# Values and output projection of two token tiles at once, by seven part products from blocks kept in DRAM

## The chip, the cores and the metric

The kernel runs on one core of a Trainium2 chip. The metric is the device time of one execution in microseconds (us): 2246.51 us before the change, the median of three runs (2245.76 to 2247.95).

## What is computed

Eight batches of 1024 tokens with 512 features go through a layer norm, then through attention with 16 heads of 32 features and through a gate with weights of plus and minus one. All of it is float32.

```python
xn = layernorm(x)                                   # x: (8, 1024, 512)
q, k, v = (heads(xn @ W.T + b) for W, b in ...)     # 16 heads of 32
scores = q @ k.T / sqrt(32)                         # masked where i % 256 < j % 256
attn = softmax(scores) @ v
s = attn @ Wo.T + bo
g = silu(clip((xn @ sign(fw).T) * scale + bias, -100, 100))
out = x + s * g
```

## The kernel before

**Tiles.** Tokens are taken in tiles of 128 (`it` = 0 to 7 of a batch `b`), heads in groups of four (`g` = 0 to 3). Every float32 product is issued as four matmuls of 32 output rows each, which lie side by side in TensorE's columns (`product`, L339); 512 columns wide, such a set of four is one of four chunks of a product, and the planner books it at 0.86 us (L382, L405). `values_work` (L373) makes the values of one token tile: four chunks into one PSUM bank, then one copy by ScalarE (L377). `output_work` (L711) makes the output of one token tile: four chunks, then on VectorE the bias (L722) and the gate (L723), on GpSimd the residual (L724), and a DMA out (L725).

**Steps.** The attention runs in 288 steps, nine for each batch and head group (L1053). In a step, `probs_quad` (L571) computes scores into a PSUM tile of four banks, called `t`, and ScalarE takes the exponential of it (L612); `attend_quad` (L618) multiplies the probabilities of the step before with the values; `maxima_quad` (L494) computes the scores `s` of the next head group into a PSUM tile of the same pool, and VectorE reduces them to maxima (L528). That pool, `ps_q`, has one buffer (L111): `t` cannot be started before the reduction of the previous `s` has ended, nor `s` before the exponential of `t`.

**What fills the gaps.** Between `t` and `s`, and between `s` and the next `t`, TensorE gets other work: the products for q, k, the values V, the output O, the gate G, and transposes. The strings STEADY, OPENING and CLOSING (L787 to L804) give the order of this filler work for each batch and head group; `V4` is the values of token tile 4, a stroke marks the batch after. `Beside.fill` (L919) deals it out: 1.2 us of booked cost between `t` and `s` (L1094), and at least 2.35 or 2.45 us between `s` and the next `t` (L1126). Works that cost no TensorE time are put off (`kept`, L1095) until after the reduction has been issued (L1122).

**Buffers and queues.** All filler products share two PSUM banks (`ps_t`, L113). GpSimd adds the probabilities of the steps up (L643); a probability tile, of which there are two (L104), comes free when that add has read it. The head groups' results `aT` are divided by VectorE (L700, four reciprocals of 128 columns) and multiplied (L704). All loads and stores of the loop are issued on SP's queue. Each engine runs its instructions in the order in which the code emits them.

Of the kernel before, what the change touches and what calls it, by code (L numbers as in the profile page):

```python
# [9 lines left out]
F32 = mybir.dt.float32  # L10
# [63 lines left out]
def tile_gated_window_attention(  # L74
# [27 lines left out]
    qk = pool("qk", 3)  # L102
    heads = pool("heads", 6)
    probs = pool("probs", 2)  # L104
    total = pool("total", 1)
    tmp = pool("tmp", 5)
    parts = pool("parts", 1)
    rows_p = pool("rows", 1)
    small = pool("small", 4)
    spill = pool("spill", 2, space=bass.MemoryType.DRAM)  # L110
    ps_q = pool("ps_q", 1, space=PSUM)  # L111
    ps_a = pool("ps_a", 2, space=PSUM)
# [128 lines left out]
    def turn_weight(name):  # L241


        def turn(c):
            if c == 0:
                wT[name] = const.tile(
                    [P, NC, D], F32R if name == "fw" else F32, name=f"{name}T"
                )
            dst = wT[name]
            if name == "wk" and c % 2:  # L250

                ps = ps_a.tile([P, 512], F32, tag="av", name=f"wkT_{c}")
            else:
                ps = bank(f"{name}T_{c}")
            for o in range(NC):
                nc.tensor.transpose(
                    ps[:, o * P : (o + 1) * P], staged[name][o][:, c * P : (c + 1) * P], ident
                )
            if name == "fw":

                sg = temp(f"sign_{c}")
                nc.vector.tensor_scalar(sg, ps, 0.0, 2.0, ALU.is_ge, ALU.mult)
                nc.vector.tensor_scalar(dst[:, c, :], sg, -1.0, None, ALU.add)
            elif name == "wo":

                nc.scalar.mul(dst[:, c, :], ps, 0.5)
            elif name == "wk":
                nc.scalar.copy(dst[:, c, :], ps)
            else:
                evacuate(dst[:, c, :], ps)  # L270

        return [lambda c=c: turn(c) for c in range(NC)]


# [97 lines left out]

    def values_work(b, it):  # L373
        def after(ps):

            vt[b, it] = vpool.tile([P, D], F32, tag="v", name=f"v_{b}_{it}")
            nc.scalar.copy(vt[b, it], ps)  # L377

        return product(
            f"v_ps_{b}_{it}",  # L380
            [(lambda c=c: (xn_cols(b, it)[:, c, :], wT["wv"][:, c, :])) for c in range(NC)],
            0.86,  # L382
            after,
            lambda: (b, it) in turned,
        )

    def heads_work(b, g, half, which):
# [20 lines left out]
        )  # L408

    def gate_work(b, it, plain=False):  # L410

# [4 lines left out]

        def split():
            src = xn_cols(b, it)
            for i in range(2):
                part[i] = parts.tile([P, NC, P], F32R, tag=f"x{i}", name=f"x{i}_{b}_{it}", bufs=2)  # L420
            nc.scalar.copy(part[0], src)  # L421
            nc.gpsimd.tensor_tensor(part[1], src, part[0].bitcast(F32), ALU.subtract)  # L422
# [21 lines left out]
        def passes(i):  # L444
# [3 lines left out]
            for c in range(NC):  # L448
# [3 lines left out]
                )  # L452
            if i:
                after(hold[0])

# [22 lines left out]
        )  # L478
        split = Work(0, split, ready=lambda: (b, it) in turned)
        return split, [main], squash, finish  # L480


# [215 lines left out]
    def invert(b, g, f, part):  # L698
        r = aT[b, g, f][:, part * P : (part + 1) * P]
        nc.vector.reciprocal(r, r)  # L700

    def normalise_heads(b, g, f, part=None):
        cols = slice(0, HALF) if part is None else slice(part * P, (part + 1) * P)
        nc.vector.tensor_tensor(  # L704
# [3 lines left out]

    back = {}

    def output_work(b, it):  # L711
# [7 lines left out]
        def after(ps):  # L719
# [6 lines left out]

        pairs = [
            (lambda g=g: (aT[b, g, it // 4][:, (it % 4) * P : (it % 4 + 1) * P], wT["wo"][:, g, :]))
            for g in range(NC)
        ]  # L730
        return fetch, product(f"o_ps_{b}_{it}", pairs, 0.86, after, lambda: it in back, True)

    def last_output(b, it):
# [8 lines left out]
        def rest():  # L742
            for part, queue in enumerate((nc.sync, nc.scalar)):
                at = slice(part * 256, part * 256 + 256)
                ps = bank(f"o_ps_{b}_{it}_{part}")
                for g in range(NC):
                    for h in range(NH):
# [3 lines left out]
                            lhsT=aT[b, g, it // 4][:, cols],  # L751
                            rhs=wT["wo"][:, g, at],
                            start=(g == 0),
# [9 lines left out]
    def row_work():  # L763
# [7 lines left out]
        def after(ps):  # L771
            nc.vector.scalar_tensor_tensor(rows["bo"], rows["bo"], 0.5, ps, ALU.mult, ALU.add)

        return spread, product(
            "bo_ps", [(lambda c=c: (wide[0][:, c, :], wT["wo"][:, c, :])) for c in range(NC)], 0.86, after,
            lambda: bool(wide), True,
        )
# [7 lines left out]


    STEADY = (  # L787
        "V4 G2 V5 q20 | V7 G3 V6 k20 q21 G4 k21",
        "O4 G5 O5 | q30 N0 k30 O6 q31 G6 k31 G7",
        "N1 O7 O0 | O1 k00' V0' q00' O2 O3 q01'",  # L790
        "k01' V1' | q11' G0' V2' k10' G1' V3' k11' q10'",
    )
    OPENING = (
        "V2 G0 V3 V4 G1 V5 V7 V6 G2 k20 q21 k21",
        "G3 q20 q30 N0 k30 | G4 q31 G5 k31 G6 V0'",
        "G7 N1 V1' | k00' q00' W0 V2' W1 V3' W2 q01' W3",
        "k01' G0' R | q11' k10' G1' k11' q10'",
    )
    CLOSING = (
        "V4 V5 | q20 V7 V6 k20 q21 k21",  # L800
        "O4 O5 | q30 k30 O6 q31 O7 k31",
        "H2 O0 H3 O1 H4 O2 H5 O3 H6 H7 |",
        "-",
# [15 lines left out]

    blocks, links = [], []  # L820

    def link(i, fn, tail=False):
        links.append((i, fn, tail))

    def plan(b, g, text):
        for word in text.split():
# [24 lines left out]
            elif kind in "qk":  # L851
                main = heads_work(bb, int(number[0]), int(number[1]), kind)
            elif kind == "V":
                main = values_work(bb, int(number))
            elif kind == "W":
                main = [Work(0.5, turn_weight("wo")[int(number)], edge=True)]
            elif kind == "R":
                spread, main = row_work()
                link(i - 3, spread)
            elif kind == "O":  # L860
                fetch, main = output_work(b - 1, int(number))
                link(i - 1, fetch)
            else:
                split, main, squash, finish = gate_work(bb, int(number), kind == "H")
                if split is not None:
                    link(i - 3, split)
                later = 1 if b in (0, B - 1) else 0
                link(i + 2 + later, squash)
# [163 lines left out]

    wv_turns, fw_turns = turn_weight("wv"), turn_weight("fw")
    start = heads_work(0, 0, 1, "k")
    start += woven(heads_work(0, 1, 1, "q"), wv_turns[:2])
    start += woven(heads_work(0, 1, 0, "k"), wv_turns[2:])
    start += values_work(0, 0)
    start += woven(heads_work(0, 1, 1, "k"), fw_turns[:2])
    start += woven(heads_work(0, 1, 0, "q"), fw_turns[2:])
    start += values_work(0, 1)  # L1040
    start = Beside(start, [0] * NQ)
# [12 lines left out]
    for s, (b, g, n) in enumerate(steps):  # L1054
# [12 lines left out]
        def fill(want, kept=None, turns=1):  # L1067

            spent = 0.0
            for one in line:  # L1070
                if spent < want - 0.1:
                    spent += one.fill(want - spent, kept, one is not now, turns)
                if one.work:
                    break
# [17 lines left out]
        if first:  # L1092
            shift_rows(*turn)
        want = max(1.2 - mine, 0.0) if nxt else share  # L1094
        spent = fill(want, kept, 0)  # L1095
        if nxt and spent < want - 0.5:
            spent += fill(want - spent, kept)
        share -= spent
        if turn and not first:
# [49 lines left out]
    for i, it in enumerate(order):  # L1149
# [8 lines left out]
        if it == order[-2]:  # L1158
            ahead, rest = last_output(b, order[-1])
            ahead()  # L1160
        for w in units[it][1]:
            w.run()

# [44 lines left out]
```

## Time and profile before

| What | us |
|---|---|
| median of three runs | 2246.51 |
| the profiled execution itself | 2248.59 |
| its span, first to last instruction | 2246.7 |
| steps begin at | 80.1 |
| a batch in the steady state (from the first `t` of one to that of the next) | 271.3 to 271.8 |
| one step of these, mean | 7.5 |
| exponential of a full `t` (L612) | 1.88 |
| reduction of a full `s` (L528, 128x2048) | 2.29 |

The span divides into 80 us of preparation, 288 steps, and some 35 us of output for the last batch. An engine's busy time is the union of its instructions; TensorE's matmuls overlap, so the mean duration of one matmul in a row is more than what it adds to the time. How far apart sets of four start is the better measure, and it is read from the timeline.

### The profile page before, as it was taken

The numbers are of one execution on the slowest core, as the hardware profiler recorded it, in microseconds if no ns is written. First come the engines' busy times: TensorE is split into PE (matmuls) and PEld (weight loads), VectorE is DVE, ScalarE is ACT, GpSimd is POOL, SyncE is SP. The second block draws the span as 40 slices with busy tenths as digits, with TensorE's granted clock in tenths as the row PEclk, the third lists the DMA queues.
The fourth block names the chain that finished last, engine by engine and source line by source line (L and its number), as shares of the span: only waits on it lengthen the run. The fifth ranks groups of instructions, "written<-read, shape, count | busy, mean of one in ns | idle before, by whom it ended". The sixth has DMA issues, their size and how long they took to land. (4 is left out here: it accounts for less than half of the span.)

```text
span 2246.7 us, 56396 instructions
## 1 busy us (share of the span) xinstructions
PE 2196.6 (98%) x25553; PEld 851.8 (38%) x25553; DVE 1276.6 (57%) x1633; ACT 876.5 (39%) x864; POOL 1323.7 (59%) x1198
## 2 busy tenths in 40 slices
PE   8999999999999999999999999999999999999998
PEld 3334333343333433333333333334333343333333
DVE  4556556665556655566555665565655665555664
ACT  2235433434334434344333443334334344333331
POOL 1256566666566666576556665557666566655562
PEclk9999999999999999999999999999999999999999
DMA  4001000120001210012000120002100111000113
GB/s 164 1 16 34 11 6 29 53 76 30 25 25 39 72 33 25 25 62 68 16 25 25 62 67 16 25 26 66 62 16 27 41 62 62 7 20 25 44 53 123
DMA packets 49672, 93.55 MB, mean 42 GB/s; under 512 B 5388, under 2 KB 5656, under 8 KB 49432
## 3 DMA queue, kind: packets, MB, share of 16 engines
q1 hardware_dynamic: 48720, 88.76, 12.0%
q8 instruction: 200, 3.28, 0.6%
q10 hardware_dynamic: 712, 1.19, 0.2%
q14 instruction: 40, 0.33, 0.0%
HBM read 56.37 MB, written 33.55 MB: 40 GB/s over the span
## 5 line engine op out<-in xcount | busy, mean ns | idle before, releaser
L643 POOL TENSOR_TENSOR p<-p,p 128x512 f32<-128x512 f32 x930 | 1096.4, 1212 | 202.7 <-PE av L625 111.2
L528 DVE TENSOR_REDUCE pm<-s 128x4 f32<-128x2048 f32 (+3 forms) x384 | 664.9, 1752 | 608.8 <-PE s L515 605.9
L612 ACT ACTIVATE p<-t 128x2048 f32<-128x2048 f32 x288 | 540.9, 1878 | 856.4 <-PE t L599 797.8
L700 DVE RECIPROCAL aT<-aT 128x128 f32<-128x128 f32 x256 | 230.2, 928 | 222.4 <-ACT aT L661 222.4
L515 PE MATMUL s<-k,q 32*128 32x512 f32 (+3 forms) x3072 | 320.2, 510 | 7.8 <-ACT p L612 6.9
L625 PE MATMUL av<-p,v 128*32 128x512 f32 (+3 forms) x3072 | 308.2, 496 | 1.6 <-DVE aT L704 1.4
L599 PE MATMUL t<-q,k 32*128 32x512 f32 (+3 forms) x3072 | 306.1, 492 | 0.0
L351 PE MATMUL q_ps<-xnT,wqT 128*32 128x512 f32 (+2 forms) x2656 | 254.2, 497 | 5.5 <-ACT xnT L322 4.7
L351 PE MATMUL k_ps<-xnT,wkT 128*32 128x512 f32 (+2 forms) x2784 | 257.2, 487 | 1.1 <-ACT xnT L322 0.7
L351 PE MATMUL v_ps<-wvT,xnT 128*32 128x512 f32 (+3 forms) x2712 | 254.9, 491 | 0.0
L351 PE MATMUL o_ps<-woT,aT 128*32 128x512 f32 (+2 forms) x2584 | 244.6, 501 | 1.7 <-ACT xnT L322 0.7
L724 POOL TENSOR_TENSOR s<-s,xb 128x512 f32<-128x512 f32 x63 | 85.8, 1362 | 245.3 <-DVE s L723 245.3
L428 POOL TENSOR_SCALAR y<-y 128x512 f32<-128x512 f32 x64 | 39.6, 619 | 279.9 <-DVE y L427 265.2
L422 POOL TENSOR_TENSOR x<-xnT,x 128x512 fp32r<-128x512 f32 x58 | 74.0, 1277 | 166.4 <-ACT x L421 164.0
L599 PEld LDWEIGHTS t<-q,k 32*128 32x128 f32 x3072 | 139.1, 185 | 25.8
L351 PEld LDWEIGHTS k_ps<-xnT,wkT 128*32 128x32 f32 x2784 | 82.7, 110 | 170.4 <-issue 142.5
L351 PEld LDWEIGHTS q_ps<-xnT,wqT 128*32 128x32 f32 x2656 | 78.3, 109 | 177.3 <-issue 152.5
L625 PEld LDWEIGHTS av<-p,v 128*32 128x32 f32 x3072 | 70.3, 108 | 195.9 <-issue 163.4
L351 PEld LDWEIGHTS v_ps<-wvT,xnT 128*32 128x32 f32 x2712 | 78.6, 109 | 167.8 <-issue 143.9
L515 PEld LDWEIGHTS s<-k,q 32*128 32x128 f32 x3072 | 116.3, 185 | 59.4 <-ACT p L612 47.5
L449 PE MATMUL y_ps<-fwT,x 128*128 128x512 f32 x464 | 135.5, 418 | 1.7 <-ACT k L394 1.3
L351 PEld LDWEIGHTS o_ps<-woT,aT 128*32 128x32 f32 x2584 | 76.2, 109 | 156.7 <-issue 135.2
(95 smaller groups left out, 1465.2 us busy)
## 6 DMA issues: line engine op xcount, KB each, us to landing
x<-in_L_attn_x_dram SPq DMA_DIRECT2D x64, 256.0 KB, 3.2
g<-t SPq DMA_DIRECT2D x64, 256.0 KB, 2.0
gb<-g SPq DMA_DIRECT2D x64, 256.0 KB, 3.1
xb<-in_L_attn_x_dram SPq DMA_DIRECT2D x64, 256.0 KB, 3.1
out_dram<-s SPq DMA_DIRECT2D x63, 256.0 KB, 2.5
wk_st<-in_L_attn_Wk_dram ACTq DMA_DIRECT2D x2, 512.0 KB, 5.5
wq_st<-in_L_attn_Wq_dram SPq DMA_DIRECT2D x2, 512.0 KB, 4.6
wv_st<-in_L_attn_Wv_dram SPq DMA_DIRECT2D x2, 512.0 KB, 6.4
```

The lines of the kernel that those rows point to most:

```text
L351: nc.tensor.matmul(hold[0][cols, lo:hi], lhsT=lhsT[:, cols], rhs=rhs[:, lo:hi], start=(i == 0 and lo == 0), stop=(i == n - 1), skip_group_ ...
L422: nc.gpsimd.tensor_tensor(part[1], src, part[0].bitcast(F32), ALU.subtract)
L428: nc.gpsimd.tensor_scalar(y[0], y[0], MAX_VAL, -MAX_VAL, ALU.min, ALU.max)
L449: nc.tensor.matmul(hold[0], lhsT=part[i][:, c, :], rhs=wT["fw"][:, c, :], start=(i == 0 and c == 0), stop=(i == 1 and c == NC - 1),)
L515: nc.tensor.matmul(sc[:, h, at : at + w], lhsT=qt[b, g][head_rows(h), i * P : (i + 1) * P], rhs=kt[b, g][head_rows(h), lo:hi], start=not f ...
L528: nc.vector.tensor_reduce(pm[:, 0 if lo == 0 else 1, i, :], sc[:, :, at : at + w], AX.X, ALU.max)
L599: nc.tensor.matmul(sc[:, h, at : at + w], lhsT=kt[b, g][head_rows(h), j * P : (j + 1) * P], rhs=qt[b, g][head_rows(h), q0 : q0 + w], start ...
L612: nc.scalar.activation(pt[:, :, :width], sc[:, :, :width], AF.Exp, scale=SCALE)
L625: nc.tensor.matmul(av[b, g, f][head_rows(h), lo : lo + w], lhsT=vt[b, j][:, g * P + h * DK : g * P + (h + 1) * DK], rhs=pts[b, g, n][:, h, ...
L643: nc.gpsimd.tensor_tensor(t[:, hs, lo : lo + w], t[:, hs, lo : lo + w], p[:, hs, at : at + w], ALU.add)
L700: nc.vector.reciprocal(r, r)
L724: nc.gpsimd.tensor_tensor(s, s, xr, ALU.add)
```

## The change

Two token tiles make a pair. With the tokens of the pair and the 512 features each halved, the product of a pair is a 2 by 2 block product. It was eight block products of 256 features by 256 columns; it is now seven, on sums and differences of the blocks (Strassen's form, as Winograd wrote it). The differences of the left side (T1 to T4) are made for each pair by VectorE; those of the weights (S1 to S4) are made once. The seven part products are collected in four PSUM banks in sequence (`phases`): two in each of the first three, one in the last; ScalarE copies the first three to SBUF (`raw_copy`), and VectorE adds them up. Wv and Wo take turns in one SBUF tile of eight blocks: after the first use they are stored in DRAM and loaded again, each once in every batch (`keep_blocks`, `load_blocks`, 1.83 MB a load). To make room, `heads` has 5 buffers, not 6, and the gate's split parts one buffer each, not two. The last batch's output after the steps stays with plain products. The order of the filler work is written anew.

```diff
-    heads = pool("heads", 6)
+    heads = pool("heads", 5)
+    raw = pool("raw", 3)
+    sums_p = pool("sums", 1)
+    wvo = pool("wvo", 1)
+    kept_w = pool("kept_w", 1, space=bass.MemoryType.DRAM)
...
+    def load_blocks(name, last=False):
+        n = len(BLOCKS)
+        wb_tile(name)
+        nc.sync.dma_start(wb["tile"].rearrange("p n c e -> p n (c e)"), block_d[name][:, 0:n, :])
...
+            phases = (
+                (("X11", "A11"), ("X22", "S4")),
+                (("T2", "S2"), ("T3", "S3")),
+                (("T1", "S1"), ("T4", "A22")),
+                (("X21", "A12"),),
+            )
...
+                for q in range(NH):
+                    cols = head_rows(q)
+                    nc.tensor.matmul(
+                        hold[k][cols, part * 256 : part * 256 + 256],
+                        lhsT=self.chunk(lhs, c)[:, cols], rhs=wb[rhs][:, c, :],
+                        start=(part == 0 and c == 0), stop=(c == 1), skip_group_check=True,
+                    )
...
+    def values_pair(b, i, j):
+        def first_sums():
+            plus(r[1][:, LO], r[0][:, LO], r[1][:, LO])
+            plus(r[1][:, HI], r[1][:, LO], r[1][:, HI])
+        def more_sums():
+            for it in (i, j):
+                vt[b, it] = vpool.tile([P, D], F32, tag="v", name=f"v_{b}_{it}")
+            plus(vt[b, i][:, HI], r[1][:, HI], r[2][:, HI])
+            plus(vt[b, j][:, HI], r[1][:, HI], r[2][:, LO])
+            plus(r[2][:, LO], r[1][:, LO], r[2][:, LO])
+            plus(vt[b, j][:, LO], r[2][:, LO], r[0][:, HI])
...
+    def output_pair(b, i, j):
+        def finish(it):
+            nc.vector.tensor_tensor(s[it], s[it], io["gb", it], ALU.mult)
+            nc.gpsimd.tensor_tensor(s[it], s[it], io["xb", it], ALU.add)
+            nc.sync.dma_start(tokens(out, b, it), s[it])
+        def first_sums():
+            plus(r[1][:, LO], r[0][:, LO], r[1][:, LO])
+            both = r[0].rearrange("p (n e) -> p n e", n=2)
+            plus(both, both, rows["bo"][:, LO].unsqueeze(1).to_broadcast([P, 2, 256]))
+            plus(r[1][:, HI], r[1][:, LO], r[1][:, HI])
+            plus(r[1][:, HI], r[1][:, HI], rows["bo"][:, HI])
+        def more_sums():
+            for it in (j, i):
+                s[it] = temp(f"s_{b}_{it}")
+            plus(s[j][:, HI], r[1][:, HI], r[2][:, LO])
+            plus(r[2][:, LO], r[1][:, LO], r[2][:, LO])
+            plus(s[j][:, LO], r[2][:, LO], r[0][:, HI])
+            finish(j)
+            fetch("xb", i)
+            plus(s[i][:, HI], r[1][:, HI], r[2][:, HI])
...
     STEADY = (
-        "V4 G2 V5 q20 | V7 G3 V6 k20 q21 G4 k21",
-        "O4 G5 O5 | q30 N0 k30 O6 q31 G6 k31 G7",
-        "N1 O7 O0 | O1 k00' V0' q00' O2 O3 q01'",
-        "k01' V1' | q11' G0' V2' k10' G1' V3' k11' q10'",
+        "V45 G2 | q20 V67 Lo G3 k20 q21 G4 k21",
+        "O45 G5 O67 | q30 N0 k30 q31 G6 k31 N1 G7",
+        "O01 O23 Lv | k00' q00' k01' q01'",
+        "V01' G0' | q11' V23' k10' G1' k11' q10'",
     )
...
+        defer[0] = kept
         spent = fill(want, kept, 0)
         if nxt and spent < want - 0.5:
             spent += fill(want - spent, kept)
+        defer[0] = None
```

`defer` puts the sums of a bank that closes between `t` and `s` after the reduction; the sums of a bank that closes later are emitted at once. `then_prepare` (not shown) puts the differences of the next pair behind the third bank of the present one, also without TensorE cost.

## The prediction, made before the changed kernel had run

> **What bounds the kernel now.** I read the page first.
>
> ```profile
> PE 2196.6 (98%) x25553; PEld 851.8 (38%) x25553; DVE 1276.6 (57%) x1633; ACT 876.5 (39%) x864; POOL 1323.7 (59%) x1198
> ```
>
> TensorE is busy for 98% of the span, VectorE for 57%. So less TensorE work should shorten the kernel, as long as TensorE stays the engine that everything waits for. Next, the waits, which tell how far the two other rings of a step are from taking over:
>
> ```profile
> ACT p L612 <- PE t L599: 797.8, 266, 5.9
> DVE pm L528 <- PE s L515: 605.9, 194, 11.0
> ...
> PEld L577 <- DVE pm L528: 26.6, 65, 1.5
> ```
>
> The exponential (L612) and the reduction (L528) wait for TensorE, by 3 us each; TensorE waits for the reduction only 26.6 us in all. But that third line is the weak point: `t` and `s` share one PSUM buffer. A step is a ring: `t` 1.3 us, exponential 1.88, `s` 1.15, reduction 2.29, with hand-overs some 6.95; TensorE's own work makes it 7.5. The slack is 0.5 us a step. Then I looked for a place where VectorE was late already, and found one in the first batch; VectorE's timeline:
>
> ```profile
> 217.61 1.75 DVE L528 TENSOR_REDUCE pm<-s 128x4 f32<-128x1536 f32 x1
> 219.39 0.19 DVE L542 TENSOR_REDUCE m<-pm 128x16 f32<-128x32 f32 x1
> ...
> 220.65 0.94 DVE L700 RECIPROCAL aT<-aT 128x128 f32<-128x128 f32 x1
> 221.50 1.28 DVE L435 SCALAR_TENSOR_TENSOR t<-t,y 128x512 f32<-128x512 f32 x1
> 222.71 1.75 DVE L700 RECIPROCAL aT<-aT 128x128 f32<-128x128 f32 x2
> 224.38 0.67 DVE L426 TENSOR_TENSOR y_ps<-y_ps,fscale_r 128x512 f32<-128x512 f32 x1
> 225.08 0.69 DVE L427 TENSOR_TENSOR y<-y_ps,fbias_r 128x512 f32<-128x512 f32 x1
> 225.69 2.28 DVE L528 TENSOR_REDUCE pm<-s 128x4 f32<-128x2048 f32 x1
> ```
>
> and TensorE's:
>
> ```profile
> 224.39 2.46 PE L351 MATMUL v_ps<-wvT,xnT 128*32 128x512 f32 x24
> 228.02 0.40 PE L577 MATMUL t<-shift,neg 3*128 3x512 bf16 x4 [1.17 <-DVE pm L528]
> ```
>
> Between two reductions VectorE had 6.33 us of other work (219.36 to 225.69), and TensorE then stood idle for 1.17 us. So up to 6.33 - 1.17 = about 5.15 us of VectorE work between two reductions is free, and each us beyond is a us of the kernel. In the steady batches of before, rows times counts give at most 4.9 us for any step. Those steps are full, though the average says 57%.
>
> **The change part by part.** The order of the built program gives the counts.
>
> *TensorE, removed.* Timelines of the tail:
>
> ```profile
> 2230.06 3.64 PE L351 MATMUL o_ps<-woT,aT 128*32 128x512 f32 x32 [0.16 <-DVE aT L704]
> ...
> 2237.77 2.37 PE L749 MATMUL o_ps<-woT,aT 128*32 128x256 f32 x40 [1.49 <-DVE aT L704]
> ```
>
> A chunk is two passes of four records. Eight passes of 512 columns in 3.64, less the last one's own 0.6, are 0.43 us a pass; ten passes of 256 in 2.37, less 0.4, are 0.217. A pair falls from 16 passes of 0.43 (6.88) to 28 of 0.217 (6.07): 0.81 us. There are 32 pairs of values and 28 of outputs: 60 x 0.81 = 49 us. TensorE also changes its tiling (32-column, 32-row, whole array) 1333 times, not 1395; such a change costs some 0.115 us (a 512-column pass is followed after 0.545, not 0.43): 7 us. Together -56.
>
> [...] The 256-column row above shows half the 512-column pass, hence hidden loads. I take the row.
>
> *VectorE, added.* A pair of values gets 10 operations of 256 columns between SBUF tiles and one that reads PSUM, where ScalarE had done it alone. A pair of outputs gets 8 of 128, 7 of 256 and 3 of 512 between SBUF tiles and one from PSUM, in place of four of 512 from PSUM (0.69 each). Nearest rows: 0.68 us for 512 columns (L435 undisturbed), 0.425 for 256 (L758 undisturbed), 0.29 for 128 (L704 on 128); in a row they overlap a little, as the reciprocals show (1.75 for two of 0.93). I take 0.68, 0.40, 0.28. That is +4.4 us a pair of values, 7.5 - 2.8 = +4.7 a pair of outputs, 37 us a steady batch. By the average nothing happens: VectorE at 57% goes to some 70%. But it comes in clumps: sums of one pair, differences of the next and the finish stand in one block between two reductions. Windows over 5.15 us in a steady batch:
> - O45 ends (g=1, first step): seven small reductions 1.26, three reciprocals 2.6, four sums 1.6, one from PSUM 0.42, two gates 1.36, eight differences 2.24, L603/L604 1.3: 10.8, over by 5.6.
> - O67 ends (g=1, third step): eight sums 3.2, three of 512 2.0, eight differences 2.24, a gate finish 0.68, a reciprocal 0.87: 9.0, over by 3.9.
> - O01 ends (g=2, second step): 7.8, over by 2.7. O23 ends (third step): 6.6, over by 1.5.
> - Three with reciprocals or values sums: 5.75, 5.55, 5.8, over by 1.6 together.
>
> 15.3 us a steady batch; six such batches, and some 10 each in the first and last: +112. Nothing else is late in these windows that would absorb it: TensorE is in order behind L577.
>
> [...] Reading two SBUF tiles costs VectorE more than its own time while GpSimd runs: L435 took 0.63 to 0.69 us alone, 2.31 at most, 0.839 in the mean, and the 1.28 in the block above is such a case; L722 and L723, one input in PSUM, never left 0.67 to 0.72. [...] By the row each operation waits 0.16 us on average, 100 operations a batch: 16 us[...]. Below, none: in the output blocks GpSimd, in order, itself waits for VectorE's gate products before it can go on with the adds. I take half the row's, 8 us a batch in full windows: +55 (0 to 112 for the range).
>
> *GpSimd and ScalarE behind it.* Where GpSimd's residual waits for the late gate product, its four adds (4 x 1.28) start late; a probability tile comes free later, and the exponential two steps on waits. Before has 58.5 us of such waits. I take +2 to 3 a batch, +20 (0 to 60). ScalarE gets 116 more copies of 0.585 us, 68 us if all delayed an exponential; it idles 3 us before each one: 0.
>
> *Floor of the ring.* With less filler, steps come down to the ring's 6.95 us; in the first and last batch and a few steady steps some of the saving falls below it: +12.
>
> *Loads.* 1.83 MB per load. At the 164 GB/s of the page's first slice 11 us. It is issued when the last values product has read the tile, and some four steps (29 us) come before O45; so nothing, and if that cover were gone, 14 x 11 = 150. Only later SP transfers queue behind its issue. Preparing and storing the blocks: four sums of 0.7 us twice, +3, mostly beside other work.
>
> *Two banks.* A bank now fills in 1.7 us, not 3.4, and the fourth bank is held until VectorE's last sum. In the long blocks TensorE waits for that bank instead of for the reduction, in the same window, so not counted twice.
>
> Sum against the profiled execution: 2248.6 - 56 + 112 + 55 + 20 + 12 = 2392, less some 10 for waits for VectorE and GpSimd that before already has and that the new order drops: 2382. From the two disputed terms[...] I take 15 off, a fifth, since some of these waits fall into windows that are not full: 2367, and 2 less for the median (2246.5 beside the profiled 2248.6): 2365.
>
> **The rivals.**
> - *TensorE stays the bound* (0.12). If the blocks are shorter than I count, say because successive sums overlap to half their duration so that no window exceeds 5.15 us, the -56 stand but for the floor: 2246 - 56 + 12, 2202, up to 2245 where a little is given back. For it: busy shares and the slack of 3 us before each reduction. Against: the 1.17 us line.
> - *A mild loss* (0.12): the blocks count[...], and half of the smaller excesses vanish: 2250 to 2300.
> - *My forecast* (0.60): 2300 to 2450.
> - [...] 2450 to 2600. The deciding point is whether L453 and L512 means come out near 0.4 or near 1.
> - *No difference* (0.02): gain and stalls cancel. A measurement of this kernel tells 0.2% (4.5 us) from no change.
>
> The range reaches into both neighbours: 2230 to 2470 leaves 0.08 below and 0.11 above. Faster 0.12, same 0.02, slower 0.86.
>
> **What would show it.** Right: L709 and L758 in the waits, with TensorE waiting for the reduction for over 100 us, in the first three steps of g=1 and g=2; VectorE near 70%, TensorE's share below 95%; 256-column passes 0.217 us apart; the mean of L453's SBUF rows above 0.42. The loads' step is right if TensorE shows no wait for DMA in the loop. Wrong: blocks between reductions at most some 5 us long, or TensorE waiting mainly for ScalarE, the load or a PSUM bank.

## The result, and the profile after

| | before | after |
|---|---|---|
| median (us) | 2246.14 (2243.2 to 2247.95) | 2543.12 (2536.13 to 2547.93) |
| profiled execution, its span (us) | 2248.59, 2246.7 | 2540.69, 2538.9 |
| mean granted clock of TensorE | 0.996 | 0.949 |
| a steady batch (us) | 271.3 to 271.8 | 307.8 to 309.3 |

After takes 1.1321 times as long (95% interval 1.1290 to 1.1352): 297 us more, where the prediction had 119 more. The direction was right; the time lies outside the range of 2230 to 2470. The page's first part, and the row of the granted clock:

```profile
PE 2248.3 (89%) x27513; PEld 943.8 (37%) x27513; DVE 1650.9 (65%) x2419; ACT 941.0 (37%) x982; POOL 1334.9 (53%) x1198
...
PEclk9999999899998999989999999999999999999989
```

TensorE's share of the span fell from 98 to 89%, while its busy time rose by 52 us, although it has less to do. The second line says why these go together: in before every slice stood at 9; here 4 show 8. The trace's clock records have 54 stretches (3 before) in which the granted clock is 0.50, most 3.4 or 6.8 us long; TensorE is busy for 214.1 us of them (10.8 before). In them the 256-column passes stand 0.427 us apart, elsewhere 0.216, so half of that busy time counts as lost. So a span can be divided into three terms: what TensorE has to do at full clock, its idle time, and half of its busy time at half clock.

| | span | idle (span less busy) | lost at half clock | work (the rest) |
|---|---|---|---|---|
| before | 2246.7 | 50.1 | 5.4 | 2191.2 |
| after | 2538.9 | 290.6 | 107.1 | 2141.2 |
| difference | +292.2 | +240.5 | +101.7 | -50.0 |

The arithmetic that the change saves is all there, 50 us of the 56 predicted. It was lost almost five times over in waiting, and twice over in what waiting does to the clock. What TensorE waits for, from the waits of TensorE alone (us in total, times, longest):

```profile
PE t L758 <- DVE pm L709: 94.4, 50, 6.9
...
PE sum L847 <- DVE s L453: 30.1, 6, 5.0
...
PE mT_ps L736 <- DVE s L453: 27.6, 7, 4.2
...
PE xnT_ps L391 <- ACT o_r L525: 23.5, 6, 5.5
...
PE s L696 <- ACT p L793: 17.8, 8, 2.9
PE o_ps L475 <- DVE o_t L512: 14.5, 6, 2.4
```

The first is the wait that the prediction named. In before the same row of matmuls was small (the prediction read the row of weight loads, 26.6 us, which is 71.4 in after):

```profile
PE t L577 <- DVE pm L528: 2.0, 3, 1.2
```

The second, third and sixth are waits for a sum or difference on VectorE that stand elsewhere in the step, and the fourth is a PSUM bank that ScalarE empties late. The timeline of one place in a steady batch shows how they follow on one another (start, duration, and in brackets the idle time before it with its releaser). First the step in which O45 ends; it takes 13.2 us, where the mean was 7.5:

```profile
1086.38 0.42 DVE L453 TENSOR_TENSOR s<-o_ps,o_r 128x256 f32<-128x256 f32 x1
...
1086.85 0.38 PE L736 MATMUL mT_ps<-identb,mt 128*128 128x128 bf16 x4 [3.90 <-DVE s L453]
...
1087.16 1.86 PE L696 MATMUL s<-k,q 32*128 32x512 f32 x8
...
1090.43 2.28 DVE L709 TENSOR_REDUCE pm<-s 128x4 f32<-128x2048 f32 x1
```

VectorE's block between two reductions, 1079.33 to 1090.43, is 11.1 us long (predicted 10.8). TensorE does not wait at its end: the next `t` starts at 1092.76 behind other work. It waits in the middle, 3.90 us, for the bank that the last sum reads; only then does it reach `s`, and computes it in 1.86 us where it takes 1.14 elsewhere. The reduction still starts as soon as VectorE's block ends. So this step is 5.7 us over the mean, 3.9 of them idle time, and the prediction had counted 5.6 for it. Two steps on, where O67 ends, it is otherwise; the step takes 14.3 us:

```profile
1107.25 1.93 PE L847 MATMUL sum<-p,ones 128*32 128x512 f32 x8 [5.01 <-DVE s L453]
...
1107.74 0.69 DVE L612 SCALAR_TENSOR_TENSOR t<-t,y 128x512 f32<-128x512 f32 x1
...
1109.16 1.26 POOL L921 TENSOR_TENSOR s<-s,xb 128x512 f32<-128x512 f32 x1 [3.96 <-DMA xb<-in_L_attn_x_dram]
...
1110.18 1.69 PE L696 MATMUL s<-k,q 32*128 32x512 f32 x8
...
1111.94 2.29 DVE L709 TENSOR_REDUCE pm<-s 128x4 f32<-128x2048 f32 x1 [1.14 <-PE s L696]
...
1113.66 14.77 POOL L824 TENSOR_TENSOR p<-p,p 128x512 f32<-128x512 f32 x12
...
1114.50 1.04 PE L780 MATMUL t<-q,k 32*128 32x512 f32 x8
...
1118.65 1.88 ACT L793 ACTIVATE p<-t 128x2048 f32<-128x2048 f32 x1 [8.83 <-POOL p L824]
...
1120.59 1.16 PE L696 MATMUL s<-k,q 32*128 32x512 f32 x8 [2.86 <-ACT p L793]
```

The same bank wait, 5.01 us, and half clock with it (`sum` takes 1.93, elsewhere 1.04). Here it costs more than VectorE's block alone: VectorE's sums and products end at 1108.43, but TensorE, held up at `sum`, reaches `s` only at 1110.18, and the reduction starts at 1111.94. Then a second chain begins. GpSimd's residual waits 3.96 us for `xb` to land, since the load of `xb` of the second tile is issued only behind the store of the first; twelve additions of probabilities queue up behind it (14.77 us). The exponential could start when its `t` is done, at 1115.54; it gets a probability tile only at 1118.65, 3.1 us late, and TensorE waits 2.86 us for it.

### The profile page after: what moved, and what is told of

Its sections match the earlier page's. It is cut to its first block, busy times and chain, and to the rows that moved or that the text cites. A ratio compares the mean times of both kernels' runs of the same rounds, so it can differ in the third digit from the quotient of the medians.

```text
span 2538.9 us, 61472 instructions
## 1 busy us (share of the span) xinstructions
PE 2248.3 (89%) x27513; PEld 943.8 (37%) x27513; DVE 1650.9 (65%) x2419; ACT 941.0 (37%) x982; POOL 1334.9 (53%) x1198
## 4 chain that ended last, share of the span: by engine, by line
PE 57%; DVE 26%; issue 5%; ACT 5%; POOL 4%; DMA 1%; ACTq 0%; DVEq 0%; SPq 0%; POOLq 0%
PE s L696 8%; PE t L780 8%; DVE pm L709 8%; PE q_ps L421 8%; PE av L806 8%; PE k_ps L421 8%; PE v_ps L475 5%; DVE aT L881 3%; PE t L758 3%; PE y_ps L626 3%; DVE v_t L509 3%; ACT p L793 3%; DVE o_r L453 2%; POOL p L824 2%; PE o_ps L475 2%
## 5 line engine op out<-in xcount | busy, mean ns | idle before, releaser
L824 POOL TENSOR_TENSOR p<-p,p 128x512 f32<-128x512 f32 x930 | 1108.6, 1222 | 317.6 <-PE av L806 212.4
L696 PE MATMUL s<-k,q 32*128 32x512 f32 (+3 forms) x3072 | 332.6, 527 | 18.6 <-ACT p L793 17.8
L780 PE MATMUL t<-q,k 32*128 32x512 f32 (+3 forms) x3072 | 328.0, 522 | 0.0
L806 PE MATMUL av<-p,v 128*32 128x512 f32 (+3 forms) x3072 | 327.7, 524 | 0.2 <-ACT p L793 0.2
L421 PE MATMUL k_ps<-xnT,wkT 128*32 128x320 f32 (+3 forms) x2728 | 265.1, 506 | 6.7 <-ACT xnT L392 5.4
L421 PE MATMUL q_ps<-xnT,wqT 128*32 128x512 f32 (+3 forms) x2776 | 261.9, 492 | 2.3 <-DVE v L453 1.4
L921 POOL TENSOR_TENSOR s<-s,xb 128x512 f32<-128x512 f32 x56 | 74.6, 1332 | 318.3 <-DVE s L920 233.6
L758 PE MATMUL t<-shift,neg 3*128 3x512 bf16 (+3 forms) x1536 | 117.7, 337 | 97.9 <-DVE pm L709 94.4
L475 PE MATMUL v_ps<-wv_blocks,v_t 128*32 128x256 f32 x2048 | 128.1, 383 | 6.0 <-DVE v_t L509 5.7
L475 PE MATMUL o_ps<-wo_blocks,o_t 128*32 128x256 f32 x1792 | 115.2, 393 | 14.5 <-DVE o_t L512 14.5
L758 PEld LDWEIGHTS <-neg 3*128 3x128 bf16 x1536 | 39.6, 92 | 222.5 <-issue 142.3
```

Source lines behind the costliest of these rows:

```text
L421: nc.tensor.matmul(hold[0][cols, lo:hi], lhsT=lhsT[:, cols], rhs=rhs[:, lo:hi], start=(i == 0 and lo == 0), stop=(i == n - 1), skip_group_ ...
L475: nc.tensor.matmul(hold[k][cols, part * 256 : part * 256 + 256], lhsT=self.chunk(lhs, c)[:, cols], rhs=wb[rhs][:, c, :], start=(part == 0 ...
L696: nc.tensor.matmul(sc[:, h, at : at + w], lhsT=qt[b, g][head_rows(h), i * P : (i + 1) * P], rhs=kt[b, g][head_rows(h), lo:hi], start=not f ...
L758: nc.tensor.matmul(sc[:, h, at : at + w], lhsT=neg1[r, :], rhs=shift[b, g, f][r, lo : lo + w], start=(k == 0), stop=False, skip_group_chec ...
L780: nc.tensor.matmul(sc[:, h, at : at + w], lhsT=kt[b, g][head_rows(h), j * P : (j + 1) * P], rhs=qt[b, g][head_rows(h), q0 : q0 + w], start ...
L806: nc.tensor.matmul(av[b, g, f][head_rows(h), lo : lo + w], lhsT=vt[b, j][:, g * P + h * DK : g * P + (h + 1) * DK], rhs=pts[b, g, n][:, h, ...
```

## The experiments

Every kernel ran once with a profile, beside a run of before on the same chip (2246.1 to 2246.5 each time). Repeated runs of after lie within 0.3% of its median, so differences under 8 us are not read. All are divided as above:

| kernel | time | span | idle | lost at half clock | work |
|---|---|---|---|---|---|
| after | 2543.1 | 2538.9 | 290.6 | 107.1 | 2141.2 |
| no_sums | 2371.3 | 2369.5 | 172.7 | 62.4 | 2134.4 |
| no_sums_ahead | 2302.2 | 2300.4 | 123.1 | 43.3 | 2134.0 |
| no_vector_pool | 2283.2 | 2281.4 | 102.2 | 45.6 | 2133.6 |
| no_differences | 2439.2 | 2437.5 | 228.5 | 67.6 | 2141.4 |
| no_pool_adds | 2424.4 | 2422.7 | 206.0 | 77.6 | 2139.1 |
| early_bank | 2584.0 | 2582.2 | 299.9 | 147.7 | 2134.6 |
| early_fetch | 2531.0 | 2529.0 | 278.9 | 107.8 | 2142.3 |
| no_loads | 2543.0 | 2541.2 | 290.1 | 110.9 | 2140.2 |
| values_plain | 2357.5 | 2355.7 | 147.6 | 44.1 | 2164.0 |
| values_spread | 2348.1 | 2346.3 | 141.5 | 38.4 | 2166.4 |
| block_10 | 2297.8 | 2296.0 | 88.4 | 15.4 | 2192.2 |
| block_14 | 2413.8 | 2412.0 | 158.2 | 62.8 | 2191.0 |
| block_14_fed | 2445.7 | 2443.9 | 92.0 | 13.5 | 2338.4 |
| block_14_fed3 | 2393.0 | 2391.2 | 117.5 | 15.1 | 2258.6 |

The last column stays within 9 us for all kernels with the pairs of after, whatever they wait for, and within 1.2 for before and the two blocks: the division holds.

### VectorE's work taken out

**no_sums** leaves out differences and sums; the bank copies of ScalarE stay, and it copies the fourth bank too.

```diff
-            for out, a, b in (
-                ("T1", "X12", "X11"), ("T2", "X22", "T1"), ("T3", "X22", "X12"), ("T4", "X21", "T2"),
-            ):
...
+            for name, of in (("T1", "X12"), ("T2", "X22"), ("T3", "X22"), ("T4", "X21")):
+                t[name] = t[of]
...
-                if k:
-                    later(first_sums if k == 1 else more_sums)
```

> Leaves out of the changed kernel all differences and sums of the pairs on VectorE (the part products use the tiles themselves; ScalarE copies the banks to where they are read), so its output is another function; matmuls, banks, loads and order of the filler work stay. Theory A (VectorE's blocks hold up TensorE, through the reductions and through the PSUM banks, and the clock that falls after each idle stretch multiplies it): TensorE is the bound again, 2190 to 2230 us, granted clock 0.99 or more. Rival B (the pair form itself: short passes, the new order of the filler, fewer buffers): still over 2400. Rival C [...]: like A here.

172 us came back, about what the prediction had put down for VectorE's blocks and for its operations beside GpSimd (167). The expected 2190 to 2230 was missed by far: without differences and sums the kernel is still 125 us slower than before. So a second cause exists. Its timeline:

```profile
1026.20 0.60 SPq L913 DMA_DIRECT2D out_dram<-s  x1
...
1026.90 0.54 SPq L903 DMA_DIRECT2D xb<-in_L_attn_x_dram  x1
...
1031.32 1.27 POOL L912 TENSOR_TENSOR s<-s,xb 128x512 f32<-128x512 f32 x1 [5.15 <-DMA xb<-in_L_attn_x_dram]
...
1032.75 1.04 PE L771 MATMUL t<-q,k 32*128 32x512 f32 x8
...
1035.82 7.36 POOL L815 TENSOR_TENSOR p<-p,p 128x512 f32<-128x512 f32 x6
...
1040.77 1.88 ACT L784 ACTIVATE p<-t 128x2048 f32<-128x2048 f32 x1 [11.61 <-POOL p L815]
```

It is the fetch: the load is issued at 1026.90, behind the store, and GpSimd, in order, stands 5.15 us in front of it. The `t` of the next step is done at 1033.79; its exponential starts at 1040.77, 7.0 us late (ScalarE was idle for 11.61 us by then).

**no_differences** keeps the sums.

> Leaves out only the differences T1 to T4 of each pair (the part products use the tiles themselves); all sums stay. Theory A: the blocks between two reductions lose 2.2 to 3.5 us of their 7 to 11, so about half of the stalls go: 2370 to 2430 us, clock between 0.96 and 0.98. Rival C: 12 of some 25 operations with two SBUF inputs per pair go, so half as well, 2400. Rival B: no change, over 2500.

2439, 9 us above the expected range: taken out of after alone, the differences are worth 104 us, more than half of the 172 that VectorE's whole added work is worth.

### The fetch and GpSimd

**no_sums_ahead** is no_sums with a fourth buffer for residual and gate, so that all four tiles of a group are fetched ahead. **early_fetch** is after with the fetch of the second `xb` moved to right behind VectorE's product of the first tile.

```diff
-    xres = pool("xres", 3)
+    xres = pool("xres", 4)
...
+            fetch("xb", i)
```

> As no_sums (no differences and sums), and with a fourth buffer for the residual and gate tiles, so that all four tiles of a pair are fetched ahead; in no_sums the second residual is fetched only when GpSimd has finished the first tile. If that fetch, which holds GpSimd's queue for some 5 us, then the exponential two steps on, is what kept no_sums at 2371 us: 2200 to 2250 us, granted clock 0.985 or more. If the pair form itself is slow (short passes, order, fewer buffers): 2340 us or more.

> The changed kernel with one line moved: the second residual's fetch is issued right behind VectorE's product that frees its buffer, not behind the first tile's store, which waits for GpSimd. Same work. If the fetch's round trip matters beside VectorE's blocks: some 1.5 to 2 us less for each of 28 pairs and the clock behind them, 2450 to 2510 us. If VectorE alone sets the pace: 2535 to 2550 us.

The fetch costs 69 us where VectorE's blocks are gone. In after, an earlier issue alone gains 12, little more than the noise, and misses its expected 2450 to 2510: GpSimd's waits for `xb` (53.4 us in after) are gone, but its waits for VectorE's product rose from 233.6 to 298.2 us. There the fetch comes on top only in part. no_sums_ahead did not reach the expected 2200 to 2250, so another 56 us were open.

**no_pool_adds** is after without GpSimd's additions of the probabilities, **no_vector_pool** is no_sums_ahead without them:

```diff
-                nc.gpsimd.tensor_tensor(
-                    t[:, hs, lo : lo + w], t[:, hs, lo : lo + w], p[:, hs, at : at + w], ALU.add
-                )
+                pass
```

> Leaves out GpSimd's adds of the probabilities (so the divisors are those of one part only); the residual and gate work of GpSimd stays. Theory A: only the waits of the exponential for GpSimd (131 us of ScalarE's, partly behind other stalls)[...] go, 2400 to 2480 us, and TensorE still waits over 150 us for VectorE. Rival C: most of the loss goes, under 2320 us. Rival B: over 2500.

> The pairs without differences and sums on VectorE, with all four tiles of residual and gate fetched ahead, and now also without GpSimd's additions of probabilities (L815 of no_sums, all steps but the last batch's last). Left out: differences, sums of the part products, and the sums of the softmax over keys, so the output is not the reference's. Theory that the loss consists of nothing but VectorE's blocks, the fetch behind GpSimd, GpSimd's late additions, and the lowered clock after the idle time that these make: what TensorE has to do is 2142 us, idle falls to before's 42 plus at most 15, the lowered clock costs under 12: 2190 to 2220 us. Rival, that the pairs cost something themselves on TensorE's path (the fourth bank, ScalarE's copies of 512 columns, tiles held longer): exponentials for GpSimd go, but TensorE still waits over 90 us in all: 2250 to 2300.

In after these additions are worth 119 us (2424.4, as expected), by two ways that this run does not part cleanly. One is the exponential's waits for a probability tile, in after:

```profile
ACT p L793 <- POOL p L824: 130.9, 33, 8.8
```

The other is that VectorE's operations between SBUF tiles take longer beside GpSimd's additions. Of TensorE's waits, those for the reduction fall from 94.4 to 45.9 us and the 17.8 us for the exponential go; those for the banks of the output blocks stay (30.1 and 27.6 in after, 29.6 and 27.6 here). The second way shows in the rows of operations between SBUF tiles by form (busy us and mean ns of one). After:

```profile
L509 DVE TENSOR_TENSOR v_t<-xnT,v_t 128x256 f32<-128x256 f32 x64 | 61.3, 958 | 1.1
...
L509 DVE TENSOR_TENSOR v_t<-xnT 128x256 f32<-128x256 f32 x64 | 58.2, 909 | 0.0
L453 DVE TENSOR_TENSOR v<-v_r,v_r 128x256 f32<-128x256 f32 x96 | 51.0, 558 | 2.7 <-ACT v_r L525 1.5
...
L453 DVE TENSOR_TENSOR v<-v_ps,v_r 128x256 f32<-128x256 f32 x32 | 13.0, 405 | 0.2 <-PE v_ps L475 0.2
```

and no_pool_adds:

```profile
L453 DVE TENSOR_TENSOR v<-v_r,v_r 128x256 f32<-128x256 f32 x96 | 37.0, 413 | 2.7 <-ACT v_r L525 1.5
...
L509 DVE TENSOR_TENSOR v_t<-xnT 128x256 f32<-128x256 f32 x64 | 33.2, 519 | 0.0
...
L509 DVE TENSOR_TENSOR v_t<-xnT,v_t 128x256 f32<-128x256 f32 x64 | 27.0, 422 | 1.1
```

In after the operations of L509, of 256 columns, take 0.42 us where no GpSimd instruction lies beside them (50); where one does, the 13 that started ahead of it take 0.42 as well, the 65 that started behind it 1.43 in the mean. (The mean of 519 ns in no_pool_adds is 58 operations of 0.42 and six of 1.5, beside other GpSimd work.) The form with an input in PSUM (L453, `v_ps`) takes 0.40 alone (18) and 0.41 under such additions (nine).

no_vector_pool missed the expected 2190 to 2220 as well; its rival's 2250 to 2300 held. With nothing left of VectorE's blocks, fetch and additions, the pairs, with the new order and the fewer buffers that come with them, still cost 35 us of span: 57.6 less work, 52.1 more idle, 40.2 more at half clock. Most of what is more idle lies in two kinds of wait: 42.8 us for the reduction in 24 places (2.0 in before), and 13.3 us in six places for a bank that ScalarE copies. One of the first kind, in a step whose filler behind `s` is spent:

```profile
911.56 0.40 PE L749 MATMUL t<-shift,neg 3*128 3x512 bf16 x4 [3.00 <-DVE pm L700]
```

One of the second, where a bank waits for its copy:

```profile
1059.13 2.22 ACT L379 ACTIVATE x<-x,nmr,rstd 128x512 f32<-128x512 f32 x3 [3.19 <-POOL nmr L369]
...
1061.26 0.56 ACT L515 COPY o_r<-o_ps 128x512 f32<-128x512 f32 x1
...
1061.87 0.66 PE L391 MATMUL xnT_ps<-ident,x 128*128 128x128 f32 x4 [2.23 <-ACT o_r L515]
...
1062.69 1.82 PE L771 MATMUL t<-q,k 32*128 32x512 f32 x8
```

ScalarE takes its work in order: its scaling of `x` (layer norm of the next batch) waits 3.19 us for GpSimd, the copy of the bank stands behind it, and TensorE waits 2.23 us for the bank. The next `t` then takes 1.82 us, not 1.03. The waits are short, 3.0 and 2.2 us here; over the whole kernel the half clock adds 40 us to their 52.

### The bank

**early_bank** has ScalarE copy the fourth bank out at once, so that no sum holds it (to make room, `small` has three buffers, not four).

```diff
+                fourth = quarter.tile([P, 256], F32, tag="q", name=f"{name}_r3")
+                nc.scalar.copy(fourth, ps[:, LO])
-                last = lambda: plus(s[i][:, LO], ps[:, LO], r[0][:, LO])
+                last = lambda: plus(s[i][:, LO], fourth, r[0][:, LO])
```

> The fourth bank of a pair is copied by ScalarE at once, into a tile of its own, and VectorE's last sum reads that copy; VectorE has as many operations as in the changed kernel. Theory A with the bank as the dearer half: TensorE's waits for VectorE's sums at the banks (some 85 us, and the clock behind them) go, part of it comes back as waits for the reduction: 2420 to 2490 us. If only the length of the blocks matters, the stalls move to the reduction in full: 2520 to 2550 us.

The theory that the bank is the dearer half fell: 2584, even 41 us more. TensorE's and ScalarE's waits say where the time went:

```profile
PE t L761 <- DVE pm L712: 158.5, 66, 6.8
PE o_ps L476 <- DVE y L607: 26.7, 6, 4.5
```

```profile
ACT p L796 <- POOL p L827: 193.8, 38, 15.3
```

The waits for the bank became waits for the reduction (158.5 us, 94.4 in after) and for a bank that VectorE's gate work holds (26.7), and GpSimd is later (193.8, 130.9 in after). The idle time in all hardly changed: 299.9 us, 290.6 in after. The block on VectorE is what has to be waited for; the bank only decides where. The 41 us are the clock (147.7 us lost, 107.1 in after): the waits are longer, 2.4 us for a mean wait for the reduction (66 of them) against 1.9 (50). The edit also has a smaller `small`, 60 more copies on ScalarE and a last sum that reads two SBUF tiles; their parts were not separated.

### What a block costs by itself

**block_10** and **block_14** are the kernel before with ten or fourteen further VectorE instructions of 0.67 us behind the sixth reduction of three head groups of each batch, 24 places in all; nothing reads their result.

```diff
+            if n == 5 and g < 3:
+                for _ in range(14):
+                    nc.vector.bn_stats(idle_st, rows["fscale"])
```

> The kernel before, with ten statistics operations on a constant (one SBUF input, 0.674 us each by its row) put on VectorE behind one reduction in each of 24 head groups, in a window that was empty: 6.7 us, 1.6 us over the free 5.15. By the window alone: 24 x 1.6 = 38 us, 2285 us. If idle stretches under 2 us leave the clock alone, the granted clock stays at 0.99 or more.

> The same with fourteen: 9.4 us, 4.3 us over. By the window alone: 24 x 4.3 = 103 us, 2350 us. If each idle stretch of that length also halves the clock for 3.4 to 6.8 us, each costs 1.7 to 3.4 us more: 2390 to 2430 us, granted clock 0.95 to 0.97.

Both agree with what was expected: the clock is 0.992 and 0.969, block_14 is in its range, and block_10 is 13 us above its sum. The free window of 5.15 us is confirmed: block_14's 14 x 0.67 = 9.4 us are 4.3 over, 24 times is 103, and idle time rose by 108. But the time rose by 167: the lost clock adds 57. block_10, whose excess is 1.6 us a place (38 in all), got 38 of idle and only 10 of clock. So an excess of 1.6 us cost 1.3 times its length (51 us for 38), and one of 4.3 us 1.6 times (167 for 103).

Does the idle time cause the lost clock, or do they only come together? **block_14_fed** adds an unused product behind the filler of those 24 steps, so that TensorE works while VectorE's block runs on.

```diff
+        if nxt and n == 5 and g < 3:
+            warm_ps = bank(f"idle_ps_{b}_{g}")
+            for _ in range(7):
...
+                    nc.tensor.matmul(
+                        warm_ps[head_rows(q), :], lhsT=wT["wq"][:, 0, head_rows(q)],
+                        rhs=wT["wq"][:, 0, :], start=True, stop=True, skip_group_check=True,
```

> The kernel before with the 14 further VectorE instructions in 24 windows (block_14: 2413.8 us, TensorE idle 150.6 us, 125.5 us of its busy time at half clock), and in each of these 24 steps an unused product of seven passes of 512 columns (3.0 us at full clock) as last filler ahead of the wait for the reduction. Nothing of the computation is left out; 72 us of TensorE work are added. Theory that half clock follows an idle stretch of over 2 us: the idle stretches of 3.5 to 6 us shrink to 0.5 to 3, TensorE's added work costs nothing, and most of the 63 us for the clock come back: 2345 to 2375 us, clock 0.985 or more. Rival, that the clock falls for another reason (a longer VectorE block, the mixture of work in these steps): clock stays near 0.97, and the time stays at 2405 to 2430. If the added passes are not hidden: above 2440.

> As block_14_fed, with three chunks in each of the 24 steps, not seven. A chunk is two passes, 0.86 us together, so block_14_fed had added 6.0 us a step, more than the stall it was to fill; three chunks are 2.6 us a step and 62 us in all. Nothing of the computation is left out. Theory that half clock follows an idle stretch of over 2 us: idle stretches of 3.5 to 6 us become 1 to 3.4 us, those under 2 keep the clock, so that of block_14's 63 us for the clock 40 to 60 come back although TensorE has more to do: 2352 to 2378 us, clock 0.98 or more. Rival, that the clock falls with VectorE's longer blocks whatever TensorE does: 2405 to 2430 us, clock 0.97 or less.

The first was mis-sized: seven chunks are fourteen passes and 6.0 us, so TensorE became the bound (work +147). The second answers. A stall of block_14, from TensorE's timeline:

```profile
1017.55 0.61 PE L578 MATMUL t<-shift,neg 3*128 3x512 bf16 x4 [4.15 <-DVE pm L529]
...
1018.05 2.02 PE L600 MATMUL t<-q,k 32*128 32x512 f32 x8
```

and of block_14_fed3 at the same place:

```profile
1016.46 0.40 PE L578 MATMUL t<-shift,neg 3*128 3x512 bf16 x4 [1.58 <-DVE pm L529]
...
1016.75 1.08 PE L600 MATMUL t<-q,k 32*128 32x512 f32 x8
```

VectorE's block is the same, TensorE has 68 us more to do, and yet the kernel is 21 us faster: 41 us of idle time are filled, and with them 48 of the 63 us lost at half clock are gone. It missed the expected 2352 to 2378 by 15, since the unused product takes a bank and waits 33.7 us in three places for VectorE's work on a gate, and 8.8 for ScalarE. That the idle time causes the half clock is shown; the rival's clock of 0.97 is out (0.988).

### Loads, and the values alone

**no_loads** leaves out the loads of the blocks in the loop, so that one set of blocks serves both products.

> The changed kernel without the loads of the weight blocks from DRAM (after the first batch both products use whatever blocks lie in the tile, so the output is another function). If the loads are hidden, as predicted: 2535 to 2550 us. If they hold up TensorE or SP's other transfers: 2500 us or less.

2543.0: the loads are hidden, as predicted.

**values_plain** has only the values in pairs, and the outputs as before; **values_spread** is the same with its filler order chosen so that no steady window of VectorE holds more than 5.15 us by count.

> Only the values are made in pairs; the output projection is plain again (eight products, its own fetch and sums as before), still from blocks loaded each batch. VectorE's windows by count: 3.3 us over 5.15 in a steady batch. TensorE's saving 32 x 0.81 = 26 us. 2246 - 26 + 23 and 10 to 20[...]: 2245 to 2275 us. If the pair form itself is slow: over 2300 us.

> The same work as values_plain with the order of the filler chosen so that no window of a steady batch is over 5.15 us by count (0.1 us over in all). By the window theory the saving shows: 2222 to 2242 us, granted clock 0.99 or more. If order is not what matters: as values_plain.

Half the change costs 102 to 111 us, for 25 to 27 us less TensorE work. Both expectations failed: values_plain lies where its rival stood, over 2300 us, and values_spread is only 9 us below it. Of the 91 us by which values_spread idles longer than before, 55 are TensorE's waits for the reduction (57.5 us, 2.0 in before). So an order that fits by count does not fit. Three steps of a steady batch have VectorE start the reduction 1.4 to 2.3 us after `s`, and the count took 0.42 us for operations that now average:

```profile
L452 DVE TENSOR_TENSOR v<-v_r,v_r 128x256 f32<-128x256 f32 x96 | 65.1, 704 | 4.1 <-ACT v_r L524 1.6
...
L452 DVE TENSOR_TENSOR v_r<-v_r,v_r 128x256 f32<-128x256 f32 x64 | 47.5, 741 | 4.9 <-ACT v_r L524 3.8
```

In after the first of these forms took 558 ns with GpSimd's additions, in no_pool_adds 413 without them. The author's estimate from that: a block that leaves the output's place falls beside such additions. This was not tried in this kernel. The other 36 us of its idle time were not traced to a cause, so that its rival, an order that does not matter, is not ruled out. None of the versions beats before.

## Why the prediction was right in direction and wrong in size

The mechanism was right: VectorE's work stands in blocks between two reductions, and TensorE waits for their excess over 5.15 us. The step that failed is the price of that wait, "each us beyond is a us of the kernel". With the half clock behind it, a us of idle time cost 1.42 (342.2 us for 240.5), and the clock has no term in the prediction. Beside it, two terms were mis-sized: GpSimd behind VectorE (+20) and the floor of the ring with ScalarE (+12 and 0). Of the signs that it named, TensorE's share below 95% (89), most means of L453 above 0.42 and no wait for a DMA in the loop came; the wait for the reduction (94 us, over 100 named) and VectorE's share (65%, near 70 named) fell a little short.

| term of the prediction | predicted (us) | more idle time | more lost at half clock |
|---|---|---|---|
| VectorE's blocks, and its operations beside GpSimd, 112 + 55 - 15 | 152 | 118 | 45 |
| GpSimd behind it: fetch of `xb`, then additions | 20 | 50 + 21 | 17 |
| floor of the ring, ScalarE | 12 | 52 | 40 |
| waits of before that the new order drops | -10 | not seen apart | |
| in all | 174 | 240.5 | 102 |

The columns of the right are read from the removals in this order: after, no_sums, no_sums_ahead, no_vector_pool, before. Another order gives other shares: the additions, taken out of after first, are worth 119 us.

- **TensorE's saving**: predicted 56 us, measured 50 by the division above, and 57 to 58 in the kernels without sums. In after the 256-column passes stand 0.216 us apart, as in the row that the prediction took (0.217).
- **The window of 5.15 us**: right. Above it idle time grows as VectorE's work does (103 expected, 108 measured in block_14).
- **VectorE's blocks, with GpSimd beside them**: taking differences and sums out gave 172 us, where the prediction had 152 to 167. That the size is near is luck: only 118 us are idle time, and 45 are the clock, which it did not have.
- **Operations on two SBUF tiles beside GpSimd**: half the row's price was too low. By the seven SBUF forms with the largest excess over 0.42 (0.28 for 128 columns), VectorE is busy 124 us longer, 15.5 us a batch: the row's full 16, not 8. The means of L453 and L512 that were to decide, 0.28 to 0.69, are far from 1; of the differences of the values (L509), at 0.91 and 0.96, that is not so. The rival of 2450 to 2600 us (0.14), the author's estimate, covers the measured time, but not by these operations, which cost 15.5 us a batch.
- **"Two banks: TensorE waits for that bank instead of for the reduction, in the same window, so not counted twice"**: this held in the block at 1079, where the reduction starts as soon as VectorE's block ends. It failed two steps on, where `s` stands behind the wait and comes so late that VectorE, done at 1108.43, starts the reduction at 1111.94. What this is worth over the whole kernel was not measured. early_bank shows that without the bank wait the idle time is the same.
- **GpSimd behind it, +20**: once VectorE's work is out, the fetch of `xb` is worth 69 us and the additions 19 more. The prediction saw the late additions, and overlooked that the load of `xb` ahead of them is issued behind a store which waits for GpSimd itself. It had counted SP's queue only for what stands behind the blocks' load.
- **Floor of the ring, +12, and ScalarE 0**: no_vector_pool shows 52 us of idle and 40 of clock. The shortest steps do come down to some 7.05 us; but where filler runs out, or where a copy stands behind a layer norm that waits for GpSimd, TensorE waits 2 to 3 us at once. At the copies it is their place in ScalarE's queue that cost time, not their length.

In sum: the prediction had 119, and the miss is 178. Of it 102 are the clock, 66 idle time, 6 the smaller saving, and the rest the difference between spans and medians. Of the 66, GpSimd and the floor have some 90 more than predicted, VectorE's blocks some 30 less, and the 10 us of dropped waits did not show. Open are the shares of VectorE's slower operations and of the late probability tile in the 119 us of the additions, those of pairs, order and buffers in what no_vector_pool still loses, and the rest of values_spread.

## What to carry to other kernels

On an engine that is in order and 98% busy, saved work is worth what it saves only if no other engine gets it as one block: list what each of the others does between two of its deadlines, and price the excess. Price a TensorE wait of over 2 us at its length and, for the half clock behind it, about half as much again: here 342 us for 240 of idle time, in block_14 165 for 108. Follow every late result one queue further, to the load that is issued behind it.

## What the runs showed of the hardware

**Half clock after short idle time.** In after, idle stretches of TensorE of 0.5 to 1 us were followed by half clock (from their start to 3.5 us behind their end) in 2 cases of 31, 1 to 2 us in 10 of 29, 2 to 3 us in 22 of 31, and 3 us or more in 26 of 27; it then lasts 3.4 us (33 stretches) or 6.8 us (19). All 12 short cases had a second idle stretch of 0.5 us or more within 3.4 us, end to start: 12 of 28 such, against none of 32 that stood alone. Its price, put at half of TensorE's busy time at the low clock, fits: with it the work of before, block_10 and block_14 comes out equal within 1.2 us.

**Useless work that pays.** 62 us of unused products in TensorE's stalls made block_14 faster by 21 us (2413.8 to 2393.0), since they shortened the idle stretches: the 26 waits for the reduction fell from 95.9 to 29.6 us, the longest from 6.0 to 3.2.

**Two SBUF inputs on VectorE beside GpSimd.** In after, for 256 columns (L509): 0.42 us alone or ahead of a GpSimd instruction, 1.43 in the mean behind one (0.93 to 1.51), mostly an addition of 1.2 us. All 28 sums of L453 that lay mostly under GpSimd's residual had started ahead of it and took 0.42. With one input in PSUM: 0.40 alone, 0.41 under an addition.
